# First batch's layer 0 in plain products, all large loads in one queue in order of use, weights' combinations beside them on two engines

## The chip, the cores and the metric

One core of a Trainium2 chip. The metric is the time of one execution on the device in microseconds (us). The kernel before takes 4024.46 us (median of 3 runs, 4024.31 to 4024.89).

Engines: TensorE (PE; PEld are its weight loads), VectorE (DVE), ScalarE (ACT), GpSimd (POOL), and SP, which here only issues transfers. Each takes its instructions in the order of the program; in the traces below an instruction of ScalarE starts 4.2 us late behind the one ahead of it, and one of VectorE stands behind 6.58 us of others. (TensorE's weight loads overlap its products.)

Words used below: a *gather* is the product with adjacency, a @ x; *turning* a block is transposing 128 rows of it on TensorE; an *eviction* copies a result of TensorE out of its accumulator memory (PSUM); the *granted clock* is the share of its full clock that TensorE had (1.00 is full), and the array is called cold when it is near 0.5; a *hole* is a stretch in which TensorE has no product; v1 is the first of v's seven pieces (explained below), n1 the turning of the normalised row block 1, counted from 0.

## The reference, cut to what matters

```python
x:   (32, 512, 512) float32     # 32 batches of 512 nodes with 512 features
adj: (512, 512) int32, about 3% ones

# layer 0
deg = a.sum(axis=1)
out = deg * (x @ Wi.T + b) + a @ (x @ Wj.T)
x   = layernorm(x + out)
# layer 1: attention with 8 heads of 64, masked by adj
q, k, v = x @ Wq.T + bq, x @ Wk.T + bk, x @ Wv.T + bv
x = layernorm(x + softmax(q k^T / 8, masked) v @ Wo.T + bo)
```

## The kernel before

The kernel works through the batches in a software pipeline. While the scores and values of batch n-1 run, the same engines make layer 0 and q, k, v of batch n. Before the first scores there is a prologue in which only batch 0 (and the gathers of batch 1) can be worked on. The change concerns this prologue.

Every 512x512 product is done in **seven pieces** of 256x256 blocks instead of eight, in the manner of Strassen and Winograd. That saves an eighth of TensorE's work, but needs sums of blocks ("combinations") of the data, made on GpSimd for each batch, and of the weights, made once, stored to DRAM and read back through a ring of 12 tiles.

The start: adjacency, x, and the weights behind them on ScalarE's queue.

```python
    for ic in range(NC):
        nc.sync.dma_start(adj_i[:, ic, :], adj[ic * P:(ic + 1) * P, :])
    wo = work([P, NC, D], "xh", 3)
    load_x(0)
    ...                                    # b0_r, bo_r: rows spread over 128 partitions, on GpSimd's queue
    adjT = turned(adj_f, big())            # 16 transposes on TensorE, evicted by ScalarE
    load_halves("wi", wiT, "k", nc.scalar)
    load_halves("wj", wjT, "oT", nc.scalar)
    pd = mm_tile("a")                      # degree sums: ones @ adjT
    ...
    ahead(0)                               # x split into two parts for the gather: ScalarE and GpSimd
    for name, src in (("wv", wvT), ("wq", wqT)):
        t = load_w(work([P, NC, D], "v", 2), src, nc.scalar)
    load_halves("wk", wkT, "q", nc.scalar)
```

The combinations of a weight, and the ring. SP's issues come in the order of the program, so a ring tile's load stands behind the stores issued before it: in the trace before, the first ring load is issued at 49.60 us, right behind wj's last stores (48.13) and a load of x (49.09).

```python
    def combine(name, eng, part):          # part 0: three operations, part 1: two
        ...
        for i, u in made:
            WS[name, i] = dram.tile([P, 2, Q], FT, name=f"{name}_{i}")
            nc.sync.dma_start(WS[name, i], u)

    def prefetch():
        while len(TILES) < min(len(KEYS), ring.used + RING) and KEYS[len(TILES)] in WS:
            t = ring_tile()
            nc.sync.dma_start(t, WS[KEYS[len(TILES)]])
            TILES.append(t)
```

The order of the prologue is `phase_a(0) + phase_b(0) + phase_c(0) + phase_a(1)`:

```python
    def phase_a(n):     # gathers of batch n, last pieces of k of batch n-1
        for i in range(max(len(g), len(k))):
            res += k[i:i + 1] + g[i:i + 1]
            if n == 0 and i == 0:
                res += [z(combine, "wj", nc.gpsimd, 0)]
            if n == 0 and i == 2:
                res += [z(combine, "wi", nc.vector, 0), z(combine, "wi", nc.vector, 1)]
            ...                            # first combinations of the data
        if g:
            res += [...]                   # the other combinations (GpSimd) and base: x += deg * b0 (VectorE)
        if n == 0:
            res += [z(combine, "wj", nc.gpsimd, 1)]
        if n == 1:
            res += [z(fold)]               # bo + Wo bv, made once
        return res
    # phase_b(0): the seven pieces of layer 0, statistics and normalisation
    # phase_c(0): turning of the normalised rows (l0_norm), pieces of v, q, k

    def fold():
        pd = mm_tile("b")
        bv_w = work([P, DC, P], "big", 6)
        for dc in range(DC):
            nc.vector.tensor_scalar(bv_w[:, dc, :], ones, bv_c[:, dc:dc + 1], None, op0=OP.mult)
            nc.tensor.matmul(pd, bv_w[:, dc, :], W["wo"][dc // 2][:, dc % 2, :], start=(dc == 0), stop=(dc == DC - 1))
        nc.vector.tensor_add(bo_r, bo_r, pd)
```

Of the kernel before, what the change touches and what calls it, by code (L numbers as in the profile page):

```python
# [9 lines left out]
FT = mybir.dt.float32  # L10
FR = mybir.dt.float32r
# [4 lines left out]
AX = mybir.AxisListType  # L16

P = 128
# [7 lines left out]
def gnn_attention_kernel(  # L26
# [51 lines left out]
    def work(shape, name, bufs, dtype=FT):  # L78
        return pools.work.tile(shape, dtype, name=name, bufs=bufs)

    def big():
        return work([P, 4, N], "big", 6)

    def mm_tile(bank):
        return psum.tile([P, 512], FT, name="mm" + bank, bufs=1)
# [19 lines left out]
    def load_x(b):  # L105
        XT[b] = work([P, NC, D], "xh", 3)
        nc.sync.dma_start(XT[b], rows(x[b]))


    def load_row(name, src):  # L110
        t = const.tile([P, D], FT, name=name)
        nc.gpsimd.dma_start(t, bass.AP(tensor=src.tensor, offset=src.offset, ap=[[0, P], [1, D]]))
        return t

    def load_col(name, src):
        t = const.tile([P, DC], FT, name=name)
        nc.gpsimd.dma_start(t, src)
        return t

    def load_w(t, src, eng):  # L120
        eng.dma_start(t, rows(src))
        return t

    adj_i = work([P, NC, N], "big", 6, I32)
    for ic in range(NC):
        nc.sync.dma_start(adj_i[:, ic, :], adj[ic * P:(ic + 1) * P, :])
    wo = work([P, NC, D], "xh", 3)
    load_x(0)
    W = {}

    def load_halves(name, src, tag, eng):

        W[name] = [work([P, 2, D], tag, 3) for _ in range(2)]
        for j in range(2):
            eng.dma_start(W[name][j], rows(src)[:, 2 * j:2 * j + 2, :])
# [4 lines left out]
    nc.gpsimd.memset(ones, 1.0)  # L140
    mhalf = const.tile([P, 1], FT, name="mhalf")
    nc.gpsimd.memset(mhalf, -0.5)
    b0_r = load_row("b0_r", b0)
    bo_r = load_row("bo_r", bo)
    bq_c = load_col("bq_c", bq)
    bk_c = load_col("bk_c", bk)
    bv_c = const.tile([P, DC], FT, name="bv_c")
    nc.gpsimd.dma_start(bv_c, bv.rearrange("(c p) -> p c", p=P))

    adj_f = big()  # L150
    for ic in range(NC):
        nc.vector.tensor_copy(adj_f[:, ic, :], adj_i[:, ic, :])

    def turned(adj_f, t):
        for jc in range(NC):
            pt = turn_tile()
            for ic in range(NC):
                nc.tensor.transpose(pt[:, ic * P:(ic + 1) * P], adj_f[:, ic, jc * P:(jc + 1) * P], ident)
            nc.scalar.copy(t[:, jc, :], pt)
        return t  # L160

    adjT = turned(adj_f, big())

    load_halves("wi", wiT, "k", nc.scalar)
    load_halves("wj", wjT, "oT", nc.scalar)
    deg_r = const.tile([P, N], FT, name="deg_r")
    pd = mm_tile("a")
    for jc in range(NC):
        nc.tensor.matmul(pd, ones, adjT[:, jc, :], start=(jc == 0), stop=(jc == NC - 1))
    nc.scalar.copy(deg_r, pd)  # L170

    told = const.tile([P, B * HP + 1], FT, name="told")
    adjR = const.tile([P, NC, N], FR, name="adjR")
    nc.vector.tensor_copy(adjR, adjT)
    deg_c = const.tile([P, NC], FT, name="deg_c")
    nc.vector.reduce_sum(deg_c, adj_f, axis=AX.X)

    SPLIT = {}

# [12 lines left out]
        split(b, 1)  # L192

    ahead(0)
    for name, src in (("wv", wvT), ("wq", wqT)):
        t = load_w(work([P, NC, D], "v", 2), src, nc.scalar)
        W[name] = [t[:, 0:2, :], t[:, 2:4, :]]
    load_halves("wk", wkT, "q", nc.scalar)


    edge = const.tile([P, NC, N], BF, name="edge")

    def graph_forms(part):
        if part == 0:
            nc.vector.tensor_tensor(adj_f, adjT, adjR.bitcast(FT), op=OP.not_equal)
        elif part == 1:
            nc.vector.reduce_sum(told[:, B * HP:], adj_f.rearrange("p c i -> p (c i)"), axis=AX.X)
            nc.vector.tensor_scalar(told[:, B * HP:], told[:, B * HP:], 2.0 * SAFE, None, op0=OP.mult)
        else:
            nc.vector.tensor_scalar(edge, adjT, 0.0, None, op0=OP.not_equal)  # L210
# [271 lines left out]
    def z(f, *a):  # L482
        return (0.0, f, *a)

    def pc(kind, b, i, bank):
        return (2 * PC if kind == "l0" else PC, piece, kind, b, i, bank)
# [4 lines left out]
    def phase_a(n):  # L491

        g = [(TR + GA, l0_gather, n, dc) for dc in range(DC)] if n < B else []
        k = [pc("k", n - 1, i, "a") for i in ORDER[2:]] if n > 0 else []
        res = []
        for i in range(max(len(g), len(k))):
            res += k[i:i + 1] + g[i:i + 1]
            if n == 0 and i == 0:
                res += [z(combine, "wj", nc.gpsimd, 0)]
            if n == 0 and i == 2:  # L500
                res += [z(combine, "wi", nc.vector, 0), z(combine, "wi", nc.vector, 1)]
            if i == 1 and g:
                res += [z(combos, TX, n, lambda j, m: quarter(XD[n], j, m), (1,)),
                        z(combos, TA, n, lambda j, m: quarter(AX_T[n], j, m), (1,))]
        if g:
            res += [z(combos, TX, n, lambda j, m: quarter(XD[n], j, m), (2,)),
                    z(combos, TA, n, lambda j, m: quarter(AX_T[n], j, m), (2,)),
                    z(base, n, 0),
                    z(combos, TX, n, lambda j, m: quarter(XD[n], j, m), (3, 4)),
                    z(combos, TA, n, lambda j, m: quarter(AX_T[n], j, m), (3, 4)),  # L510
                    z(base, n, 1)]
        if n == 0:
            res += [z(combine, "wj", nc.gpsimd, 1)]
        if n == 1:
            res += [z(fold)]
        return res

    def project(m, i):

# [7 lines left out]
    def phase_b(n):  # L527

        m = n - 2
        if m < 0:  # L530
            res = []
            side = [z(graph_forms, i) for i in range(3)] + [z(combine, name, nc.vector, i) for name in ("wv", "wq")
                                                            for i in range(2)] if n == 0 else [z(add_bo, 0, i) for i in range(2)]
            for i, bank in (ALONE[0:1] + ALONE[2:3] + ALONE[1:2] + ALONE[3:]):
                res.append(pc("l0", n, i, bank))
                if i == 4:
                    res += [z(stats, n, 0)]
                res += side[:1]
                side = side[1:]
            return res + [z(apply, n, 0), z(stats, n, 1)]  # L540
        res = []
        for i in ORDER:
            res.append(pc("l0", n, i, "a"))
            if i == 4:
                res.append(z(stats, n, 0))
            if i == 5:
                res.append(z(stats, m, 0))
            if i == 3:
                res.append(z(stats, n, 1))
            res += project(m, i)  # L550
            if i == 4:
                res.append(z(apply, n, 0))
            if i in (7, 4):
                res.append(z(add_bo, n - 1, int(i == 4)))
        return res

    def phase_c(n):

        m = n - 2
        norm = [(TR, l0_norm, n, ic) for ic in range(NC)]  # L560
        h = lambda j, i: quarter(HT[n], j, i)
        res = [norm[0], norm[1], z(apply, n, 1), pc("v", n, 1, "a"), pc("q", n, 1, "b")]
        if m >= 0:
            res += [z(stats, m, 1)]
        if n == 0:
            res += [z(combine, "wk", nc.vector, 0)]
        res += [pc("v", n, 2, "a"), norm[2], norm[3], z(combos, TH, n, h, (1, 2)), pc("k", n, 1, "a"),
                z(combos, TH, n, h, (3, 4)), pc("q", n, 2, "b"), pc("k", n, 2, "a")]
        if n == 0:
            res += [z(combine, "wk", nc.vector, 1)]  # L570
        if m >= 0:
            res += [z(apply, m, 0), z(apply, m, 1), z(store, m)]
        for i in ORDER[2:]:
            res += [pc("q", n, i, "b"), pc("v", n, i, "a")]
            if i == 5 and n + 1 < B:
                res += [z(load_x, n + 1)] if n > 0 else []
        if n == 0:
            res += [z(combine, "wo", nc.vector, 0), z(combine, "wo", nc.vector, 1)]
        if n + 1 < B:
            res += [z(ahead, n + 1)]  # L580
        return res
# [29 lines left out]
    def run(f):  # L611
        f[1](*f[2:])
# [32 lines left out]
        nc.vector.tensor_scalar(tot, pd[:, 0:1], SAFE, None, op0=OP.is_lt)  # L645
        nc.vector.tensor_scalar(again, tot, -1.0, 1.0, op0=OP.mult, op1=OP.add)

    PERIODS = [phase_a(0) + phase_b(0) + phase_c(0) + phase_a(1)]
    PERIODS += [by_steps(phase_b(n) + phase_c(n) + phase_a(n + 1)) for n in range(1, B)]
    PERIODS += [last_steps()]  # L650
    for f in PERIODS[0] + [f for p in PERIODS[1:] for todo in p for f in todo]:
# [3 lines left out]
    tot = const.tile([P, 1], FT, name="tot")  # L655
    again = const.tile([P, 1], I32, name="again")

    for i, f in enumerate(PERIODS[0]):
        if f[1] is piece and ring.used == 0:
            load_w(wo, woT, nc.scalar)  # L660
            W["wo"] = [wo[:, 0:2, :], wo[:, 2:4, :]]
            load_x(1)
            prefetch()
        run(f)
    for n in range(1, B + 1):
        b = n - 1
        extra = []
# [178 lines left out]
```

## Time and profile before

In the profiled run the first scores begin at 151.41 us. From there to the end, 31 periods and the end of the last, it takes 3873 us with TensorE 97% busy. The prediction below divides the 151.41 us before it into stretches, and shows them.

The page's rows in slices say which engine bounds. The stretches say where the prologue loses time. The chain that ended last says what a hole waits for: it is followed back from the last instruction, so its lines, read downwards, are what each next step waited for.

### The profile page before, as it was taken

How to read it: one execution, taken by the hardware profiler on the slowest of the kernel's cores; microseconds unless marked ns; L12 is line 12 of the kernel's file. 1: busy time of each engine (PE TensorE's matmuls, PEld its weight loads, DVE VectorE, ACT ScalarE, POOL GpSimd, SP SyncE). 2: the span in 40 equal slices, each digit the busy share in tenths (PEclk: the TensorE clock that was granted, in tenths of full speed). 3: DMA queues.
4: the chain of work that ended last, by engine and by line, in shares of the span. 5: the costliest groups of instructions: out<-in, count | busy, mean ns of one | idle time of the engine just before them, and what ended most of it. 6: DMA issues, size and time to landing. Idle time of an engine off the chain costs nothing.

```text
span 4024.5 us, 47060 instructions
## 1 busy us (share of the span) xinstructions
PE 3872.3 (96%) x17418; PEld 2653.4 (66%) x17418; DVE 2618.5 (65%) x3529; ACT 1059.2 (26%) x1477; POOL 1856.2 (46%) x1867
## 2 busy tenths in 40 slices
PE   6999999999999999999999999999999999999997
PEld 4666666666666666666666666666666666666663
DVE  4466666666666666666666666666666666666666
ACT  1222222223222222222222222222222222222322
POOL 4344345444445443454444454444554434544433
PEclk8999999999999999999999999999999999999998
DMA  6333333333333333333333333334333333333330
GB/s 231 115 97 111 110 118 87 113 110 107 116 105 97 114 106 110 119 99 103 110 108 113 110 94 116 106 104 123 100 102 107 113 108 118 91 111 110 105 110 22
DMA packets 284394, 437.55 MB, mean 109 GB/s; under 512 B 23296, under 2 KB 121088, under 8 KB 284160
## 3 DMA queue, kind: packets, MB, share of 16 engines
q1 hardware_dynamic: 280688, 427.65, 35.4%
q10 hardware_dynamic: 3216, 6.29, 0.4%
q8 instruction: 142, 2.33, 0.2%
q0 software_dynamic: 256, 0.53, 0.1%
q14 instruction: 92, 0.75, 0.1%
HBM read 392.96 MB, written 41.42 MB: 108 GB/s over the span
## 4 chain that ended last, share of the span: by engine, by line
PE 75%; DVE 17%; POOL 4%; issue 2%; ACT 2%; DMA 0%; SPq 0%; ACTq 0%; DVEq 0%; POOLq 0%
PE mma L372 31%; PE mmb L372 15%; PE sc L424 10%; PE ov L446 9%; PE mmb L296 6%; DVE xh L309 5%; DVE e L429 3%; DVE rl L459 3%; PE ov L453 2%; DVE es L438 2%; POOL mv L265 2%; PE sc L289 1%; POOL mv L264 1%; PE sc L317 1%; ACT sc L428 1%
## 5 line engine op out<-in xcount | busy, mean ns | idle before, releaser
L372 PE MATMUL mma<-ring,big 128*128 128x256 f32 x5288 | 1233.8, 383 | 51.3 <-DMA ring<-in_wiT_dram 23.3
L372 PEld LDWEIGHTS mma<-ring,big 128*128 128x128 f32 x5288 | 994.5, 190 | 278.0 <-DVE e L429 49.5
L428 ACT ACTIVATE sc<-sc 128x1024 f32<-128x1024 f32 x512 | 492.8, 1006 | 1546.2 <-PE sc L424 1468.1
L429 DVE TENSOR_TENSOR e<-sc,edge 128x1024 f32<-128x1024 f32 x512 | 602.4, 1217 | 368.2 <-ACT sc L428 368.1
L435 POOL TENSOR_TENSOR es<-e 128x1024 f32<-128x1024 f32 x128 | 301.4, 2354 | 895.0 <-PE ov L453 887.4
L341 POOL TENSOR_TENSOR big<-big 128x512 f32<-128x512 f32 x384 | 525.3, 1393 | 218.9 <-DVE big L290 198.2
L424 PE MATMUL sc<-q,k 64*128 64x512 f32 x2048 | 509.6, 616 | 0.2 <-ACT big L318 0.2
L446 PE MATMUL ov<-e,v 128*64 128x512 f32 x2048 | 497.2, 606 | 6.5 <-DVE told L464 6.5
L459 DVE RECIPROCAL rl<-ov 128x128 f32<-128x128 f32 x512 | 454.7, 923 | 5.3 <-PE ov L453 1.6
L372 PE MATMUL mma<-big,ring 128*128 128x256 f32 x1792 | 430.4, 383 | 27.9 <-DVE v L400 24.2
L372 PE MATMUL mmb<-big,ring 128*128 128x256 f32 x1792 | 426.6, 381 | 15.3 <-DVE q L415 15.3
L372 PEld LDWEIGHTS mma<-big,ring 128*128 128x128 f32 x1792 | 332.3, 190 | 112.2 <-DVE v L400 36.7
L372 PEld LDWEIGHTS mmb<-big,ring 128*128 128x128 f32 x1792 | 337.9, 190 | 72.8 <-DVE q L415 27.3
L264 POOL TENSOR_SCALAR mv<-mv 128x1 f32<-128x1 f32 x256 | 79.7, 311 | 622.9 <-DVE mv L263 609.1
L446 PEld LDWEIGHTS ov<-e,v 128*64 128x64 f32 x2048 | 124.7, 136 | 347.6 <-issue 294.8
L438 DVE TENSOR_TENSOR es<-es,e 128x1024 f32<-128x1024 f32 x256 | 326.1, 1274 | 4.4
L424 PEld LDWEIGHTS sc<-q,k 64*128 64x128 f32 x2048 | 176.5, 186 | 209.8 <-issue 195.2
L387 POOL TENSOR_TENSOR xh<-xh,p 128x512 f32<-128x512 f32 x189 | 234.4, 1269 | 131.0 <-ACT p L379 131.0
L390 DVE TENSOR_TENSOR xh<-xh,mma 128x512 f32<-128x512 f32 x189 | 127.5, 675 | 248.4 <-PE mma L372 220.7
L186 POOL TENSOR_TENSOR xlo<-xh,xhi 128x512 fp32r<-128x512 f32 x128 | 161.7, 1274 | 245.1 <-ACT xhi L185 245.1
L372 PE MATMUL mmb<-ring,big 128*128 128x256 f32 x1080 | 262.7, 387 | 5.8 <-POOL big L341 4.9
L269 ACT ACTIVATE xh<-xh,mv 128x512 f32<-128x512 f32 x256 | 198.5, 812 | 236.9 <-POOL mv L266 221.3
(115 smaller groups left out, 3668.5 us busy)
## 6 DMA issues: line engine op xcount, KB each, us to landing
ring<-wi SPq DMA_DIRECT2D x160, 256.0 KB, 2.6
ring<-wj SPq DMA_DIRECT2D x160, 256.0 KB, 2.7
ring<-wq SPq DMA_DIRECT2D x160, 256.0 KB, 2.7
ring<-wv SPq DMA_DIRECT2D x160, 256.0 KB, 2.6
ring<-wk SPq DMA_DIRECT2D x160, 256.0 KB, 3.9
ring<-wo SPq DMA_DIRECT2D x155, 256.0 KB, 2.6
xh<-in_x_dram SPq DMA_DIRECT2D x32, 1024.0 KB, 5.6
out_dram<-xh SPq DMA_DIRECT2D x31, 1024.0 KB, 5.1
```

The lines of the kernel that those rows point to most:

```text
L296: nc.tensor.matmul(pm, parts[w][:, jc, :], adjR[:, jc, :], start=(w == 0 and jc == 0), stop=(w == 1 and jc == NC - 1))
L309: nc.vector.scalar_tensor_tensor(y, b0_r, deg_c[:, ic:ic + 1], y, op0=OP.mult, op1=OP.add)
L341: nc.gpsimd.tensor_tensor(dst, p, q, op=OP.subtract)
L372: nc.tensor.matmul(pm[:, c * Q:(c + 1) * Q], lhs, rhs, start=first, stop=(kc == 1 and n == len(terms) - 1), skip_group_check=True)
L387: nc.gpsimd.tensor_tensor(d, d, p1, op=OP.add)
L424: nc.tensor.matmul(ps[:, s, :], KT[b, hp // 2][r, hp % 2, kc * P:(kc + 1) * P], QT[b, hp // 2][r, hp % 2, :], start=True, stop=True)
L428: nc.scalar.activation(ps, ps, AF.Exp, scale=QSCALE)
L429: nc.vector.tensor_tensor(e, ps, edge[:, kc:kc + 1, :].to_broadcast([P, 2, N]), op=OP.mult)
L435: nc.gpsimd.tensor_add(ES[hp], E[0], E[1])
L438: nc.vector.tensor_add(ES[hp], ES[hp], E[kc])
L446: nc.tensor.matmul(PV[hp][s * HD:(s + 1) * HD, :], V[b][:, kc, c0:c0 + HD], E[kc][:, s, :], start=(kc == 0), stop=(kc == NC - 1))
L459: nc.vector.reciprocal(rl[:, c], pl[:, c])
```

## The change

Its intent is that TensorE gets work as soon as the gathers are done. Layer 0 of batch 0 is multiplied out plainly, row block by row block, straight from the loaded weights, so no combination and no ring tile is needed for it. The loads are issued early, in one queue, in order of use. The weights' combinations are made while TensorE does the plain products, those of wi and wj on GpSimd and the others on VectorE. The core of the diff:

```diff
@@ start
-    wo = work([P, NC, D], "xh", 3)
     load_x(0)
...
+    load_halves("wi", wiT, "k", nc.sync)
+    load_halves("wj", wjT, "oT", nc.sync)
+    for name, src in (("wv", wvT), ("wq", wqT)):
+        t = load_w(work([P, NC, D], "v", 2), src, nc.sync)
+        W[name] = [t[:, 0:2, :], t[:, 2:4, :]]
+    load_halves("wk", wkT, "q", nc.sync)
+    load_x(1)
+    wo = load_w(work([P, NC, D], "xh", 3), woT, nc.sync)
...   # turned() also writes adjR, from PSUM; b0_r, bo_r and the columns are loaded after ahead(0)
@@ phase_a
-            if n == 0 and i == 0:
-                res += [z(combine, "wj", nc.gpsimd, 0)]
-            if n == 0 and i == 2:
-                res += [z(combine, "wi", nc.vector, 0), z(combine, "wi", nc.vector, 1)]
+            if n == 1 and i in (1, 3):
+                res += [z(combine, "wo", nc.vector, i // 2)]
...
+    def first():
+        g = [(TR + GA, l0_gather, 0, dc) for dc in range(DC)]
+        half = lambda name, i: z(combine, name, nc.gpsimd if name in ("wi", "wj") else nc.vector, i)
+        y = [(8 * PC / 4, plain, ic) for ic in range(NC)]
+        n = [(TR, l0_norm, 0, ic) for ic in range(NC)]
+        return [g[0], z(graph_forms, 3), g[1], g[2], half("wv", 0), g[3], z(base, 0, 0), z(base, 0, 1), half("wv", 1),
+                y[0], half("wq", 0), half("wi", 0), y[1], half("wq", 1), half("wi", 1), y[2], half("wk", 0), half("wj", 0),
+                n[0], y[3], half("wk", 1), half("wj", 1), n[1]]
+
+    def plain(ic):
+        pm = mm_tile("ab"[ic % 2])
+        c = slice(ic * P, (ic + 1) * P)
+        for j, (t, w) in enumerate(((XD[0], W["wi"]), (AX_T[0], W["wj"]))):
+            for dc in range(DC):
+                nc.tensor.matmul(pm, t[:, dc, c], w[dc // 2][:, dc % 2, :], start=(j + dc == 0), stop=(j == 1 and dc == DC - 1))
+        y = XT[0][:, ic, :]
+        nc.vector.tensor_add(y, y, pm)
+        mv = work([P, 5], "mv", 12)
+        ln_stats(mv, y)
+        ln_apply(mv, y)
@@ phase_c
+            side = [z(graph_forms, 2), None, z(graph_forms, 0), None, z(graph_forms, 1)]   # between pieces of q and v
@@
-    PERIODS = [phase_a(0) + phase_b(0) + phase_c(0) + phase_a(1)]
+    PERIODS = [first() + phase_c(0) + phase_a(1)]
```

More of the change, by code (lines that the diff above doesn't have):

```diff
@@ L142, in gnn_attention_kernel @@
     nc.gpsimd.memset(mhalf, -0.5)
-    b0_r = load_row("b0_r", b0)
-    bo_r = load_row("bo_r", bo)
-    bq_c = load_col("bq_c", bq)
-    bk_c = load_col("bk_c", bk)
-    bv_c = const.tile([P, DC], FT, name="bv_c")
-    nc.gpsimd.dma_start(bv_c, bv.rearrange("(c p) -> p c", p=P))
+    load_halves("wi", wiT, "k", nc.sync)
[6 more added lines that the diff above has]
+    wo = load_w(work([P, NC, D], "xh", 3), woT, nc.sync)
+    W["wo"] = [wo[:, 0:2, :], wo[:, 2:4, :]]
     adj_f = big()
@@ L152, in gnn_attention_kernel, with turned @@
         nc.vector.tensor_copy(adj_f[:, ic, :], adj_i[:, ic, :])
-    def turned(adj_f, t):
+    def turned(adj_f, t, also=None):
         for jc in range(NC):
@@ L159, in turned @@
             nc.scalar.copy(t[:, jc, :], pt)
-        return t
-    adjT = turned(adj_f, big())
-    load_halves("wi", wiT, "k", nc.scalar)
-    load_halves("wj", wjT, "oT", nc.scalar)
+            if also is not None:
+                nc.vector.tensor_copy(also[:, jc, :], pt)
+        return t
+    told = const.tile([P, B * HP + 1], FT, name="told")
+    adjR = const.tile([P, NC, N], FR, name="adjR")
+    adjT = turned(adj_f, big(), adjR)
     deg_r = const.tile([P, N], FT, name="deg_r")
@@ L169, in gnn_attention_kernel @@
         nc.tensor.matmul(pd, ones, adjT[:, jc, :], start=(jc == 0), stop=(jc == NC - 1))
-    nc.scalar.copy(deg_r, pd)
-    told = const.tile([P, B * HP + 1], FT, name="told")
-    adjR = const.tile([P, NC, N], FR, name="adjR")
-    nc.vector.tensor_copy(adjR, adjT)
     deg_c = const.tile([P, NC], FT, name="deg_c")
-    nc.vector.reduce_sum(deg_c, adj_f, axis=AX.X)
     SPLIT = {}
@@ L194, in gnn_attention_kernel @@
     ahead(0)
-    for name, src in (("wv", wvT), ("wq", wqT)):
-        t = load_w(work([P, NC, D], "v", 2), src, nc.scalar)
-        W[name] = [t[:, 0:2, :], t[:, 2:4, :]]
-    load_halves("wk", wkT, "q", nc.scalar)
+    nc.scalar.copy(deg_r, pd)
+    b0_r = load_row("b0_r", b0)
+    bo_r = load_row("bo_r", bo)
+    bq_c = load_col("bq_c", bq)
+    bk_c = load_col("bk_c", bk)
+    bv_c = const.tile([P, DC], FT, name="bv_c")
+    nc.gpsimd.dma_start(bv_c, bv.rearrange("(c p) -> p c", p=P))
     edge = const.tile([P, NC, N], BF, name="edge")
     def graph_forms(part):
-        if part == 0:
+        if part == 3:
+            nc.vector.reduce_sum(deg_c, adj_f, axis=AX.X)
+        elif part == 0:
             nc.vector.tensor_tensor(adj_f, adjT, adjR.bitcast(FT), op=OP.not_equal)
@@ L511, in phase_a @@
                     z(base, n, 1)]
-        if n == 0:
-            res += [z(combine, "wj", nc.gpsimd, 1)]
         if n == 1:
@@ L531, in phase_b @@
             res = []
-            side = [z(graph_forms, i) for i in range(3)] + [z(combine, name, nc.vector, i) for name in ("wv", "wq")
-                                                            for i in range(2)] if n == 0 else [z(add_bo, 0, i) for i in range(2)]
+            side = [z(add_bo, 0, i) for i in range(2)]
             for i, bank in (ALONE[0:1] + ALONE[2:3] + ALONE[1:2] + ALONE[3:]):
@@ L561, in phase_c @@
         h = lambda j, i: quarter(HT[n], j, i)
-        res = [norm[0], norm[1], z(apply, n, 1), pc("v", n, 1, "a"), pc("q", n, 1, "b")]
+        res = [norm[0], norm[1], z(apply, n, 1)] if n else []
+        res += [pc("v", n, 1, "a"), pc("q", n, 1, "b")]
         if m >= 0:
             res += [z(stats, m, 1)]
-        if n == 0:
-            res += [z(combine, "wk", nc.vector, 0)]
         res += [pc("v", n, 2, "a"), norm[2], norm[3], z(combos, TH, n, h, (1, 2)), pc("k", n, 1, "a"),
                 z(combos, TH, n, h, (3, 4)), pc("q", n, 2, "b"), pc("k", n, 2, "a")]
+        side = []
         if n == 0:
-            res += [z(combine, "wk", nc.vector, 1)]
+            side = [z(graph_forms, 2), None, z(graph_forms, 0), None, z(graph_forms, 1)]
         if m >= 0:
@@ L573, in phase_c @@
         for i in ORDER[2:]:
-            res += [pc("q", n, i, "b"), pc("v", n, i, "a")]
+            for f in pc("q", n, i, "b"), pc("v", n, i, "a"):
+                res += [f] + [g for g in side[:1] if g]
+                side = side[1:]
             if i == 5 and n + 1 < B:
                 res += [z(load_x, n + 1)] if n > 0 else []
-        if n == 0:
-            res += [z(combine, "wo", nc.vector, 0), z(combine, "wo", nc.vector, 1)]
         if n + 1 < B:
@@ L656, in gnn_attention_kernel @@
     again = const.tile([P, 1], I32, name="again")
-    for i, f in enumerate(PERIODS[0]):
-        if f[1] is piece and ring.used == 0:
-            load_w(wo, woT, nc.scalar)
-            W["wo"] = [wo[:, 0:2, :], wo[:, 2:4, :]]
-            load_x(1)
+    for f in PERIODS[0]:
+        run(f)
+        if f[1] is combine:
             prefetch()
-        run(f)
     for n in range(1, B + 1):
```

## The prediction

> **What bounds the kernel now.** I read the page first, the busy rows in 40 slices of about 100 us each.
>
> ```profile
> PE   6999999999999999999999999999999999999997
> PEclk8999999999999999999999999999999999999998
> ```
>
> TensorE is the bound in every slice but the first and last: 90% or more busy. Section 1 of the page has it at 3872.3 us of 4024.5. So nearly all of the time is product work of the 32 batches, and only the 152 us in which TensorE is idle can be won by reordering. The change touches only what comes before the first scores, so I asked for the busy time of each engine in the stretches up to there (columns: window, length, busy us and count of PE, PEld, DVE, ACT, POOL, granted clock, DMA share, GB/s).
>
> ```profile
> 0.00:13.99 13.99, 4.31 (x17) 3.11 (x17) 1.98 (x4) 3.04 (x4) 4.00 (x13) 1.00 0.63 188
> 13.99:32.47 18.48, 15.82 (x57) 9.45 (x56) 10.45 (x8) 5.01 (x9) 10.86 (x8) 1.00 0.94 340
> 32.47:55.77 23.30, 0.00 (x1) 0.00 (x1) 11.30 (x8) 0.58 (x1) 14.59 (x10) 0.53 0.55 186
> 55.77:89.45 33.68, 29.20 (x120) 24.25 (x121) 16.54 (x27) 2.68 (x4) 8.37 (x12) 0.91 0.61 205
> 89.45:138.30 48.85, 48.07 (x225) 40.96 (x224) 18.82 (x33) 11.39 (x21) 17.41 (x16) 0.97 0.65 200
> 138.30:151.41 13.11, 5.69 (x8) 2.24 (x8) 7.82 (x10) 0.00 (x0) 6.52 (x5) 0.74 0.06 20
> ```
>
> These six stretches are: adjacency load and turning; degree sums and the four gathers of batch 0; nothing at all; layer 0 of batch 0 with its normalisation; v, q, k of batch 0 and the gathers of batch 1; the folding of the last bias. TensorE does 103 us of work in 151.4 us. The largest hole is the third, 23.3 us with no product. The chain that ended last says what fills it (start, length, what).
>
> ```profile
> 28.27 4.84 DMA wj<-e
> ...
> 35.76 5.57 POOL big L341 x4
> ...
> 42.36 4.53 POOL big L341 x2
> 46.88 1.22 POOL e L233
> 48.10 0.60 POOL e L234
> ...
> 49.60 6.13 DMA ring<-in_wiT_dram
> 55.77 2.50 PE mma L372 x5
> ```
>
> Batch 0 runs layer 0 in seven products on combined operands. GpSimd has to make eight combinations of the data (L341) and those of the second weight (L233, L234); and the ring's first tiles stand in the SP queue behind the store of the last weight combination, so the first product waits for all of it. Two more stretches of the timeline matter: the late adjacency, and the price of the hole.
>
> ```profile
> 9.33 0.43 DVE L152 CAST big<-big 128x512 f32<-128x512 int32 x1 [4.43 <-DMA big<-in_adj_dram]
> 10.59 0.43 DVE L152 CAST big<-big 128x512 f32<-128x512 int32 x1 [0.83 <-DMA big<-in_adj_dram]
> ...
> 55.77 6.38 PE L372 MATMUL mma<-ring,big 128*128 128x256 f32 x16 [23.30 <-DMA ring<-in_wiT_dram]
> ```
>
> **What the Trainium skill says.** (1) "TensorE: Matmul & The Clock Gate", Part 1, on the HAM clock gate: an idle window of about 3.4 us halves the array's clock, and about as long of sustained work restores it. The trace agrees: granted clock 0.53 in the hole, and the first piece of 16 matmuls took 6.38 us where warm ones have 3.62. (2) "DMA: Bandwidth & Descriptors", section "Issuing engines are not separate DMA queues": all issuers share the same 16 engines and interleave, so more queues bring no bandwidth. The trace agrees as far as it goes: two adjacency blocks were in by 3.6 us, the others landed at 9.3 and 10.6, while the broadcast rows from GpSimd moved; the rate with ScalarE and SP queues full was 340 GB/s. (3) "GPSIMD Engine Reference", Specifications: its SBUF interfaces are shared with VectorE, with contention where VectorE reads two SBUF operands. The trace agrees: a VectorE combination of wi took 1.64 to 1.75 us beside GpSimd, one of wv 0.69 us alone.
>
> **The change, part by part.**
>
> *Start.* The rows' loads leave GpSimd's queue until after the first splits, and 9 MB go through one queue in order of use. Each SP issue costs 0.42 us, so adjacency is issued by 2.6 us; 1 MB at 310 to 370 GB/s (rates seen at 2 to 4 us) lands near 5.5. Last cast 6.0 (was 11.0). Transposes after it took 3.1 us, then degree sums 4.8 us: done at 13.9 instead of 19.0. At 340 GB/s, x follows at about 8.5, wi 11.5, wj 14.5, wv 17.5, wq 20.5, wk 23.5: each before its use below. **5 us won.**
>
> *Gathers.* Their undisturbed pitch was 2.81 us (transposes at 22.37, 25.19, 28.00); the last lost over 1.4 us because GpSimd made weight combinations between its splits. Four at 2.81 end at 13.9 + 11.2 = 25.1 (was 32.5).
>
> *Layer 0.* Four row blocks of eight 128x512 matmuls take the place of seven pieces. A warm piece has a pitch of 3.45 us for 16 records 256 wide (0.216 each); a block is 16 records 512 wide, 6.9 us by that scale. So 27.6 us for 24.2, **3.4 us more** TensorE work, but it needs no combination of data (eight GpSimd operations, about 11 us) and no ring tile, only wi, wj and the gathers, all there. The hole of 23.3 us and the cold start (6.38 - 3.45 = 2.9 us) go.
>
> *Normalisation.* Before, 81.5 to 89.5 us held a chain of statistics with some 4 us of TensorE idle. Now each block is normalised while the next is multiplied, and two turnings (0.44 each) lie between. v's first piece starts at 25.1 + 27.6 + 0.9 = 53.6. It started at 89.66 before and took 2.90 for 1.73, cold. **36 us, and 1.2 for the cold piece.** The last block's chain (add 0.69, statistics 0.9, three small GpSimd operations up to 2.7, apply 0.8: about 5 us) lies under n1, v1, q1, v2 (0.44 + 3 x 1.73 = 5.6 us). It just fits.
>
> *Combinations.* For five weights 25 operations: 15 on VectorE at 0.69 (0.42 for a negation), 10 on GpSimd at 1.28 (0.61). VectorE alone has in 13.9 to 53.6 about 2.8 (XD) + 2.3 (degree) + 9.5 (combinations) + 2.8 to 6 (base) + 6.3 (adds, statistics) = 24 to 27 us; add GpSimd's 11.4 for the shared port: 38 of 40 us at worst. Beside TensorE, not on the path.
>
> *v, q, k.* Three graph forms move here: 1.22, 3.35 and 2.28 us on VectorE between evictions. Bank a is single, and TensorE gives it 1.73 us of slack. Working the queue through, the 3.35 costs about 1.25 us, the 2.28 about 0.45. **1.7 us lost.** wo's combinations go into batch 1's gathers, where VectorE has idle stretches of 2 to 3 us: 0 to 0.5 us.
>
> *Not changed.* The fold: VectorE still does four base operations beside GpSimd (6.24 us) before it. The rest of the kernel, 31 periods: the same instructions.
>
> Sum: first scores at 53.6 + (151.48 - 89.66 - 1.17) + 1.7 + 0.3 = 116.3 instead of 151.5: **35 us, 4024.5 - 35 = 3989.5 us**, ratio 0.991.
>
> **Rivals.** (a) *VectorE or GpSimd becomes the bound of the new stage.* For it: 38 of 40 us at worst, in-order queues in which a block's add stands behind combinations, with only two banks. Against it: GpSimd is not busy all the time. It would make gaps of 5 to 10 us: 3995 to 4000. (b) *One queue delays what is needed.* Adjacency could land at 8 to 10 us again if some DMA engines lag with 9 MB behind it, or b0's row comes late among them: base, and with it the first add, waits. 2 to 5 us: 3992 to 3995. (c) *The gain is given back*, because the prologue was hidden work or later buffers come free later. Against it: TensorE is at 90% or more in every later slice and nothing later waits for a clock; a product started earlier ends earlier. It would make 4020. (d) *More is won*: if the fold's stall (7.4 us of idle, then 5.77 for 3.45 us of products) shrinks, 3983.
>
> **Range and chances.** The mechanism's core (23.3 + 2.9 of the hole and cold piece, some 8 for start and gathers, some 5 for the normalisation, less 3.4 and 2) is firm to about 8 us, and the tail is towards less gain: 3981 to 4001. Two per cent would be 80 us, more than the 48 us in which TensorE is idle before the first scores; a loss of 80 us has no mechanism. Faster 0.01, same 0.98, slower 0.01.
>
> **What would show it.** Right: degree sums end near 14 us; first plain product near 25 us with no hole before it; v's first piece near 54; first scores near 116; the granted clock near 1.00 from 20 to 54 us; the stretch from first scores to the end as long as before (3873 us). Wrong: idle of TensorE over 2 us in 25 to 54 released by VectorE's add or GpSimd's normalisation (a), by a load (b), a longer stretch after the first scores (c). What I can't see before is how the shared queue orders 9 MB, and how buffers pass from one tile to another once the order of allocation changes.

## The result, and the profile after

The changed kernel takes **3994.79 us** (median of 4 runs, 3993.80 to 3996.93) against 4024.39 (4 runs, 4023.64 to 4024.89) for the kernel before: 29.6 us less. The ratio is 0.9927, with a 95% interval of 0.991 to 0.9945. The difference is within 2%, as predicted, and inside the range. The point was 3989.5, so the change brought 5.3 us less than said.

The changed kernel's busy rows in slices of some 100 us: only the first slice differs.

```profile
PE   8999999999999999999999999999999999999997
PEclk9999999999999999999999999999999999999998
```

Its busy time in stretches (window, length, busy us and count of PE, PEld, DVE, ACT, POOL, granted clock, DMA share, GB/s):

```profile
0.00:10.54 10.54, 4.48 (x16) 3.10 (x17) 3.09 (x6) 3.04 (x4) 0.88 (x8) 1.00 0.83 262
10.54:14.11 3.57, 3.57 (x10) 1.61 (x10) 1.38 (x2) 1.62 (x3) 2.14 (x2) 1.00 1.05 394
14.11:24.78 10.67, 9.96 (x49) 7.71 (x48) 8.36 (x10) 3.38 (x6) 6.42 (x8) 1.00 1.06 371
24.78:54.15 29.37, 29.37 (x77) 13.50 (x75) 13.84 (x25) 3.50 (x5) 13.87 (x17) 1.00 0.94 336
54.15:58.10 3.95, 0.00 (x1) 0.00 (x0) 1.37 (x4) 1.28 (x2) 3.68 (x6) 1.00 0.77 293
58.10:62.48 4.38, 4.38 (x12) 3.56 (x13) 0.00 (x0) 0.59 (x1) 0.45 (x1) 0.61 0.54 184
107.35:121.14 13.79, 6.04 (x8) 2.38 (x8) 8.15 (x10) 0.00 (x0) 6.86 (x5) 0.63 0.11 38
```

Lines three and four answer to the old hole: gathers are followed at once by plain products, 29.4 us with TensorE busy throughout at full clock. The fifth line is new: 3.95 us of nothing, in the middle of v's first piece, and the sixth shows the array cold after it. The clock fell only behind the hole: windows of the same trace give 1.00 up to 58.5 and 0.50 from 59 to 62 us, so it is the work after the hole that pays. The last line is the fold, with its old idle stretch. The chain that ended last says what v's first piece waited for:

```profile
53.70 1.27 POOL e L232
...
55.05 0.63 POOL mv L267
...
55.75 0.62 POOL mv L268
...
56.47 0.28 POOL mv L269
...
56.77 0.81 ACT xh L272
57.58 0.48 ACT big L321
...
58.10 1.64 PE mma L375 x4
```

The same in order of time (start, length, operation, in brackets the idle time before it and who ended it):

```profile
52.69 0.60 PE L320 MATMUL sc<-ident,xh 128*128 128x128 f32 x4
57.49 0.56 ACT L321 COPY big<-sc 128x512 f32<-128x512 f32 x1
62.48 1.89 PE L375 MATMUL mma<-ring,big 128*128 128x256 f32 x8
```

L321 is ScalarE's eviction of the turned block 1. TensorE had turned that block by 53.3, and it has nothing to do with block 3. It has no bracket, because ScalarE did not idle before it: the instruction just ahead of it is L272, the normalisation of block 3, which waits for block 3's statistics on GpSimd. The eviction ran at 57.49 (the chain counts it from the end of L272, 57.58), though its input was there at 53.3. The third line is v's second piece, which started only at 62.48.

The chain's first line shows a smaller part: in this run GpSimd's statistics (L267) stood 0.5 us behind a weight combination (L232), though VectorE had handed over at 54.5. In four other runs with the same hole (the changed kernel again, plain products alone, weights on ScalarE's queue, the fold earlier) the hole was 3.44 to 3.45 us. So of the 3.95 us some 0.5 belong to this one run.

One number serves for the comparisons below, because it leaves out how early the adjacency lands (the first plain product began between 24.8 and 27.2 us in runs that share the changed start): **the time from v's first piece to the first scores**. It was 151.41 - 89.45 = 61.96 us before and is 121.14 - 53.12 = 68.02 us after.

### The profile page after: what moved, and what is told of

Read it like the earlier page. It is cut to its first block, busy times and chain, and to the rows that moved or that the text cites. A ratio compares the mean times of both kernels' runs of the same rounds, so it can differ in the third digit from the quotient of the medians.

```text
span 3992.5 us, 46921 instructions
## 1 busy us (share of the span) xinstructions
PE 3869.0 (97%) x17370; PEld 2641.8 (66%) x17370; DVE 2611.4 (65%) x3525; ACT 1058.9 (27%) x1476; POOL 1846.2 (46%) x1861
## 4 chain that ended last, share of the span: by engine, by line
PE 75%; DVE 18%; POOL 3%; issue 2%; ACT 2%; DMA 0%; SPq 0%; POOLq 0%
PE mma L375 31%; PE mmb L375 14%; PE sc L427 10%; PE ov L449 9%; PE mmb L299 6%; DVE xh L312 5%; DVE e L432 4%; DVE rl L462 3%; PE ov L456 2%; DVE es L441 2%; PE sc L292 1%; POOL mv L268 1%; DVE st L265 1%; POOL mv L267 1%; PE sc L320 1%
## 5 line engine op out<-in xcount | busy, mean ns | idle before, releaser
L375 PE MATMUL mma<-ring,big 128*128 128x256 f32 x5224 | 1216.3, 382 | 31.7 <-ACT p L382 20.6
L375 PEld LDWEIGHTS mma<-ring,big 128*128 128x128 f32 x5224 | 979.6, 190 | 255.9 <-DVE e L432 49.5
L344 POOL TENSOR_TENSOR big<-big 128x512 f32<-128x512 f32 x376 | 511.6, 1385 | 217.8 <-DVE big L293 195.8
L375 PE MATMUL mma<-big,ring 128*128 128x256 f32 x1792 | 430.2, 383 | 27.9 <-DVE v L403 24.2
L267 POOL TENSOR_SCALAR mv<-mv 128x1 f32<-128x1 f32 x256 | 80.8, 316 | 618.0 <-DVE mv L266 604.4
L272 ACT ACTIVATE xh<-xh,mv 128x512 f32<-128x512 f32 x256 | 198.4, 811 | 240.2 <-POOL mv L269 224.6
L375 PE MATMUL mmb<-ring,big 128*128 128x256 f32 x1032 | 251.6, 387 | 4.9 <-POOL big L344 4.9
```

Of the source, the lines that this page charges most:

```text
L344: nc.gpsimd.tensor_tensor(dst, p, q, op=OP.subtract)
L375: nc.tensor.matmul(pm[:, c * Q:(c + 1) * Q], lhs, rhs, start=first, stop=(kc == 1 and n == len(terms) - 1), skip_group_check=True)
```

## The experiments

The theory (A): the missing 5 us are the new wait, and it comes from order on ScalarE. Rival (B): the statistics' chain on GpSimd, slowed by weight combinations, is late for whatever comes next. A further question was what each part of the change was worth, and whether the fold's stall could be mended. Kernels sent together ran on the same chip in up to five rounds; all results were correct. The runs from "The start alone" on were on other chips and without the changed kernel. Where they are compared with its 3994.54 or 3994.79 us, that is across chips; the kernel before took 4024.13 to 4025.33 us there.

**The changed kernel again.**

> The changed kernel as it is, so that its variants can be compared with it on the same chip. Expected: 29 to 31 us below the kernel before (3993.5 to 3996), and again one hole of about 4 us inside v's first piece near 54 us, released by ScalarE's eviction of the turned block (L321).

3994.54 us (3993.69 to 3997.51) against 4024.66: 30.1 less. Hole of 3.44 us, v's first piece to scores 67.97 us. The result stands.

**Turning of block 1 ahead of the last block.**

```diff
-                n[0], y[3], half("wk", 1), half("wj", 1), n[1]]
+                n[0], n[1], y[3], half("wk", 1), half("wj", 1)]
```

> Turning of block 1 is put ahead of the last row block's products instead of behind them. Theory A (ScalarE takes its work in order, so block 1's eviction stands behind the last block's normalisation, and v's first piece behind both): the hole of 3.95 us and the slow first q piece (3.11 for 1.73) go, v's second piece starts at 56.5 to 57 instead of 62.5, 5 to 6 us less than the changed kernel in the same call. Rival B (the statistics on GpSimd, delayed by its weight combinations, are what is late for whatever comes next): the wait only moves to the turning of block 3, 0 to 2 us less.

3989.52 us (3987.19 to 3990.83): 35.1 less than before, 5.0 less than the changed kernel. v's first piece to scores is 62.86 us, 5.1 shorter. This variant's TensorE and ScalarE in order of time:

```profile
57.40 0.82 ACT L272 ACTIVATE xh<-xh,mv 128x512 f32<-128x512 f32 x1 [5.37 <-POOL mv L269]
58.13 0.56 ACT L382 COPY p<-mma 128x512 f32<-128x512 f32 x1
58.74 1.99 PE L375 MATMUL mma<-ring,big 128*128 128x256 f32 x8 [1.29 <-ACT p L382]
```

A small hole is left, and it has the same form: now the eviction of v's first piece (L382) stands behind block 3's normalisation. B had expected the wait at the turning of block 3, and 0 to 2 us. A's figure of 5 to 6 us holds at its lower edge. Its second piece of v, expected at 56.5 to 57, came at 58.74: the 1.29 us of this hole, and the 0.7 us by which the plain products began later in this run (25.49 against 24.78), are what A's working had left out.

**Combinations of wi and wj on VectorE too.**

```diff
-        half = lambda name, i: z(combine, name, nc.gpsimd if name in ("wi", "wj") else nc.vector, i)
+        half = lambda name, i: z(combine, name, nc.vector, i)
```

> wi's and wj's combinations go to VectorE too, so GpSimd has only statistics in this stage; the order of the program is kept. Theory A: block 1's eviction still stands behind the last block's normalisation, whose chain gets shorter by 0.5 to 1.5 us (about 0.5 of waiting behind L232, faster small operations): 0.5 to 1.5 us less than the changed kernel, a hole of 2.5 to 3.5 us stays. Rival B: the hole goes, 4 to 6 us less. If VectorE then becomes the bound of the stage: TensorE waits for its adds (L536), and the time is up by 1 to 5 us.

3996.08 us (3994.02 to 3996.92) against the changed kernel's 3994.54 (3993.69 to 3997.51); the ranges overlap, so no difference is shown. A hole of 3.74 us stays. B falls as the cause of the hole: with no combination left on GpSimd the wait is no shorter. My own expectation, that the chain gets shorter, missed as well: from the start of block 3's statistics to the start of its normalisation took 58.24 - 55.30 = 2.94 us here and 57.34 - 54.69 = 2.65 in the changed kernel. TensorE did not wait for VectorE's adds either, so one engine would have done. The second engine in the change's name bought nothing that these runs can show.

**Block 3's normalisation alone on VectorE.**

```diff
         ln_stats(mv, y)
-        ln_apply(mv, y)
+        if ic == NC - 1:
+            nc.vector.tensor_scalar(y, y, mv[:, 3:4], mv[:, 4:5], op0=OP.mult, op1=OP.add)
+        else:
+            ln_apply(mv, y)
```

> The last block's normalisation alone (one operation of 0.81 us) goes from ScalarE to VectorE; all orders and the statistics' chain stay as they are. Theory A: nothing stands ahead of block 1's eviction on ScalarE, it runs at about 53.3 instead of 57.5, the hole goes, 5 to 6 us less than the changed kernel, as with the turning moved. Rival B: no change, 0 to 1 us less.

3989.90 us (3989.05 to 3991.60): 4.6 less than the changed kernel. The statistics' chain is as it was, only ScalarE is free. The eviction of this variant, and TensorE behind it:

```profile
54.35 1.97 PE L375 MATMUL mma<-ring,big 128*128 128x256 f32 x8
54.55 0.59 ACT L321 COPY big<-sc 128x512 f32<-128x512 f32 x1 [2.50 <-PE sc L320]
56.16 1.89 PE L375 MATMUL mmb<-big,ring 128*128 128x256 f32 x8
57.07 1.47 DVE L540 TENSOR_SCALAR xh<-xh,mv 128x512 f32<-128x512 f32 x1 [1.32 <-POOL mv L269]
57.89 1.89 PE L375 MATMUL mma<-ring,big 128*128 128x256 f32 x8
```

L321 now waits for TensorE alone. There is no hole; v's first piece to scores is 62.21 us, 5.8 shorter. Block 3 is normalised no sooner than before, at 57.07, and nobody minds. This settles A: the chain itself could be hidden, and it was the instruction queued behind it that could not wait. "TensorE: Matmul & The Clock Gate" of the Trainium skill (Part 1, the paragraph on engine queue depths) says that only TensorE reorders, and only its weight loads, while ScalarE and VectorE are strictly first in, first out; the trace of the changed kernel agrees, with 4.2 us (57.49 against 53.3).

**The start alone.** The kernel before with the new loads and turning, layer 0 in seven pieces as before (the block of the diff's first part, and no more).

> The kernel before with the new start only: all large loads early in one queue in order of use, rows' loads later, adjacency turned into both forms at once. Layer 0 of batch 0 stays in seven pieces with combinations. Prediction's account: degree sums end at 14 instead of 19, gathers about 7 us earlier, the chain of GpSimd's combinations and ring loads shifts with them, so 5 to 8 us less than before (4016 to 4020), and the hole ahead of the first piece stays near 20 us. Rival (the loads set the hole): the hole shrinks to under 10 us, 15 us or more less.

4018.82 us (4017.20 to 4020.03) against 4024.13: 5.3 less. The hole is not shorter for it. This variant's first piece:

```profile
51.08 6.54 PE L374 MATMUL mma<-ring,big 128*128 128x256 f32 x16 [23.44 <-DMA ring<-in_wiT_dram]
```

Everything came 4.7 us earlier, the hole included. Loading earlier did not shorten the wait; the chain of combinations and ring loads made it.

**Plain products alone.** The changed kernel with the start of the kernel before.

> The changed kernel with the start of the kernel before: loads of the weights on ScalarE's queue behind the turning, rows' loads first. Layer 0 in plain products. If the two parts add up: 29.6 less 5 to 8, so 21 to 25 us less than before (3999 to 4003). If the plain products need the early loads (weights landing late at 20 to 30 us leave a hole ahead of the first block): less than 20 us less.

4001.81 us (4000.20 to 4003.38): 22.3 less. TensorE did not idle ahead of the first block (28.48 us), so the plain products don't need the early loads. The parts add up to 5.3 + 22.3 = 27.6 of the 29.6 to 30.1 measured together, which is within the spread of the runs. One caution: adjacency's last cast was at 8.30 us in this run, and at 10.59 in the profiled run of the kernel before, with the same start. That part of the start varies from run to run.

**Weights on ScalarE's queue, at the same place in the program.**

```diff
-    load_halves("wi", wiT, "k", nc.sync)
+    load_halves("wi", wiT, "k", nc.scalar)
...   # wj, wv, wq, wk, wo likewise
```

> The changed kernel with the weights' loads issued at the same place of the program but on ScalarE's queue instead of SP's, so that they compete with adjacency and x. If one queue in order of use matters: adjacency's last block lands 1 to 4 us later, ScalarE is held by issues before its first eviction, and the time is up by 2 to 8 us against the changed kernel. If only the early issue matters: within 1 us of the changed kernel.

4001.58 us (3999.68 to 4002.45): 6.8 to 7.0 above the changed kernel's two medians. ScalarE and adjacency in this variant:

```profile
8.55 3.50 ACTq L134 DMA_DIRECT2D q<-in_wkT_dram  x2
9.14 0.43 DVE L154 CAST big<-big 128x512 f32<-128x512 int32 x1 [0.82 <-DMA big<-in_adj_dram]
12.09 0.48 ACTq L121 DMA_DIRECT2D xh<-in_woT_dram  x1
13.90 1.07 ACT L161 COPY big<-sc 128x512 f32<-128x512 f32 x2
```

Two things happened, as expected. Adjacency's last cast is at 9.14 instead of 6.42, and ScalarE, busy issuing until 12.6, then loaded its function table (1.28 us, which in the changed kernel ran at 0.74) and made its first eviction at 13.90 instead of 7.41. The second is the larger. By these sizes the gain of "one queue" is mostly that SP, which computes nothing, does the waiting; no run parts the two.

**The fold earlier.** In the changed kernel the fold's operand (L611) stands on VectorE behind the four base operations (L312). These take 6.58 us beside GpSimd's combinations; batch 0's four, at 24.06 us with GpSimd idle, took 2.73. The changed kernel:

```profile
108.18 6.58 DVE L312 SCALAR_TENSOR_TENSOR xh<-b_r,deg_c,xh 128x512 f32<-128x512 f32 x4
114.68 0.86 DVE L611 TENSOR_SCALAR big<-ones,bv_c 128x128 f32<-128x128 f32 x4
115.10 6.12 PE L612 MATMUL mmb<-xh,big 128*128 128x512 f32 x8 [7.75 <-DVE big L611]
```

```diff
+        if n == 1:
+            res += [z(fold)]
         if g:
             res += [...]                   # combinations and base
-        if n == 1:
-            res += [z(fold)]
```

> The changed kernel with the fold of the last bias put ahead of batch 1's base operations and last combinations instead of behind them. From the trace: TensorE idles 7.75 us ahead of the fold and then runs it cold, 6.12 for about 3.5, because VectorE's four base operations (6.58 us beside GpSimd) stand ahead of the fold's operand. Expected: hole of 1 to 2 us, fold 3.5 to 4.5 us, 6 to 9 us less than the changed kernel. Rival: the base operations and combinations then are late for the first pieces of the next period, and the gain is given back there: 0 to 3 us less.

3988.41 us (3985.95 to 3990.78): 35.7 less than before, some 6 less than the changed kernel. The hole, expected at 1 to 2 us, is 2.08, but the fold stays slow (5.54 us, 3.5 to 4.5 expected), and the gain is just under or at the lower end of the 6 to 9 us expected. The rival, that the gain is given back later, falls: from the first scores to the end it took 3870.4 us. This variant's combinations, operand and products:

```profile
105.38 7.87 POOL L344 TENSOR_TENSOR big<-big 128x512 f32<-128x512 f32 x6 [2.42 <-DVE big L293]
108.57 4.77 DVE L611 TENSOR_SCALAR big<-ones,bv_c 128x128 f32<-128x128 f32 x4
109.82 5.54 PE L612 MATMUL mmb<-xh,big 128*128 128x512 f32 x8 [2.08 <-DVE big L611]
```

Four operations that took 0.86 us in the changed kernel took 4.77 us. GpSimd's six combinations now ran beside them; the run with the operand early, below, moves them to where GpSimd is idle, and they take 0.87. So the products came only as their operands were made, about 1.2 us apart, and the granted clock fell to 0.50 from 111 to 114 us: late operands and a cold array both lie in the 5.54 us.

**Both mends** (block 3's normalisation on VectorE, fold early).

> The last block's normalisation on VectorE and the fold ahead of base and combinations, together. If both holes are separate stalls of TensorE, their gains add: 4.6 + 6.1 under 3994.5, so 3983 to 3985. If the second only uses slack that the first makes: 3987 to 3989.

3984.24 us (3982.26 to 3985.03) against 4025.33: 41.1 less. The gains add (4.6 and 6.1 expected together, 11 found), so the two holes were separate stalls of TensorE.

**The fold's operand early.** As the last, but the operand is made during batch 1's first gather, in a buffer that is free then.

```diff
+            if n == 1 and i == 0:
+                res += [z(fold_operand)]   # the four tensor_scalar of fold(), into work([P, N], "rl", 1)
```

> The last variant with the fold's operand made during batch 1's first gather, in another free buffer (rl), and only its products after k's last piece. In the run with the early fold the operand's four VectorE operations took 4.77 us beside GpSimd instead of 0.86, so TensorE waited 2.08 us, went cold and took 5.54 for about 3.5. Expected: no hole, fold 3.4 to 3.7 us, first scores 3.5 to 4.5 us earlier, 3979 to 3981. Rival (the scores then wait for k's last eviction on VectorE, or the granted clock is low there anyway): under 2 us.

3979.97 us (3975.64 to 3981.01): 45.4 less than before, 4.3 less than with both mends. This variant:

```profile
89.17 0.87 DVE L616 TENSOR_SCALAR rl<-ones,bv_c 128x128 f32<-128x128 f32 x4
103.72 3.60 PE L623 MATMUL mmb<-xh,rl 128*128 128x512 f32 x8
107.25 1.99 PE L427 MATMUL sc<-q,k 64*128 64x512 f32 x8
```

The operand, made while GpSimd is idle, is back at 0.87 us, the products run warm in 3.60, and the scores follow at once. v's first piece to scores is 51.74 us: 16.3 us shorter than in the changed kernel.

**Graph forms in layer 0's stage.**

```diff
-            side = [z(graph_forms, 2), None, z(graph_forms, 0), None, z(graph_forms, 1)]
+            side = []                      # forms 0, 2, 1 now behind half("wv", 1), half("wi", 0), half("wi", 1)
```

> The last variant with the three graph forms on VectorE in layer 0's stage, as it had idle stretches of 3 to 4 us there, instead of between the evictions of v and q. In the changed kernel's trace two pieces start 0.3 us late each behind v's evictions, not 1.7 us in sum as predicted. Expected: about 0.6 us less, which these rounds can hardly show; the trace should show pitches of 1.73 us throughout. If a form delays a block's add or statistics: 0 to 2 us more.

3979.72 us (3978.06 to 3980.38), not to be told from the last. In the trace v's first piece to scores is 51.01 us instead of 51.74, 0.7 us shorter, and the two late pieces are gone. Both last variants beat the two kernels: ratios to before of 0.9885 and 0.9886.

## Why the prediction was right, and where it was off

*The bound and the mechanism.* Right. The hole of 23.3 us and the normalisation's idle time are gone; the first plain product follows the gathers without a pause. The plain products took 24.78 to 52.7 with one turning between them, 27.5 us (27.6 predicted). The 24.2 us of seven warm pieces, against which their cost was reckoned, no run measures by themselves.

*Start.* The sum was right by errors that cancel, and that is luck of the profiled run. Adjacency's last cast ended at 6.85 us (it began at 6.42), not at 6.0, and the transposes behind it took 3.69 us, not 3.1. But the degree sums ran warm, 3.57 us instead of 4.8. They ended at 14.1 (13.9 predicted). Gathers: 10.7 us instead of 11.2. In the nine other runs with this start the last cast began at 6.3 to 7.6 us; in the eight of them that also have the plain products, the first of these began at 25.5 to 27.2 us, where the prediction had 25.1 and the profiled run 24.78.

*Normalisation: the step that failed.* "It just fits" compared block 3's chain (about 5 us) with the 5.6 us of TensorE work behind which it was to lie. The chain's length was right: 52.9 to 57.6, so 4.7 us. But the cover was counted on TensorE alone. v1 needs the turned block 1, which ScalarE has to evict first, and the prediction never asked where in ScalarE's queue that eviction stood: behind the very chain that v1 was to cover. The term was put at 0. It measured 62.48 - 53.12 = 9.36 us for two pieces of 1.73 each, so 5.9 us: 3.95 of hole and the rest cold array. In the second profiled run of the same kernel it was 62.61 - 54.20 - 3.46 = 4.95 us, 3.44 of it the hole. The runs with block 1 turned earlier and with the normalisation on VectorE give it back (5.0 and 4.6 us). The prediction's signs of being wrong named an add of VectorE, GpSimd's normalisation or a load as the releaser; the releaser was ScalarE's eviction, and GpSimd's statistics stood only behind that.

*Combinations.* Off the path, as said. No wait of TensorE for VectorE in 25 to 53 us. The rival of a VectorE or GpSimd bound did not come; moving all to VectorE changed nothing that shows.

*v, q, k.* The graph forms were put at 1.7 us and cost 0.7 at most. The comparison with adjR took 2.28 us, not the 3.35 that the trace of before showed, where GpSimd's combinations ran beside it.

*The fold*, "not changed": 7.75 + 6.12 us instead of 7.42 + 5.77, so 0.7 us worse.

*The sum.* First scores at 121.14 instead of 116.3: the 5.9 us, less 0.5 for an earlier v, less about 1 for the forms, and 0.7 for the fold. That makes 121.4; the 0.3 left over is no larger than what the prediction had put down for wo's combinations. From there to the end the profiled runs took 3871.4 us after and 3873.1 before; over all profiled runs this rest lies between 3868.7 and 3873.9, so nothing is to be read in it. That it gives nothing back speaks against the rival (c).

*Two readings that don't hold*, neither of which enters the sum: TensorE's idle time from 81.5 to 89.5 us was 2.96 us and not some 4 (the whole stretch from 55.77 has 4.48), and the eight combinations of data took GpSimd 14.1 us, of which the last six are the 11 named.

## What to carry to other kernels

When work is said to lie under other work, walk the queue of every engine that the covering work passes through, not only the engine that is covered: one instruction that waits, ahead of an eviction in the same queue, uncovers everything. A stall of TensorE can cost more than its length, because the array comes back cold: here 3.95 us of hole cost 5.9 us, while a hole of 1.29 us left the clock at 1.00. Short operations on VectorE that are stretched beside GpSimd's work (0.86 to 4.77 us here) belong where GpSimd is quiet. Loads on a queue whose engine has nothing else to do were 7 us better here than on ScalarE's, though no run parts that from the order of the queue.

## What the Trainium skill lacked or had wrong

- "TensorE: Matmul & The Clock Gate", Part 1, gives an idle window of about 3.4 us after which the clock is halved, but not how much work inside the window keeps it up. With the fold early, TensorE was idle for only 2.08 us, and products then came about 1.2 us apart; that was enough for a granted clock of 0.50 three microseconds after the hole began. A hole of 1.29 us with dense work behind it (block 1 turned earlier) left the clock at 1.00.
- "DMA: Bandwidth & Descriptors", section "Issuing engines are not separate DMA queues", says that several issuers only save the time of issuing, "usually small relative to the DMA itself". At the start of this kernel, with several MB issued ahead, it was not small: ScalarE's two issues for wk took 3.50 us, and the six weights kept ScalarE issuing until 12.6 us, its first eviction coming at 13.90 instead of 7.41; with adjacency 2.7 us later the kernel took 7 us more.
